# A two-layer graph attention kernel: scoring and summing layer 0's large units in two parts

## Chip, cores and metric

The kernel runs on one core of a Trainium2 chip. The metric is device microseconds (us) of one execution, from start to end on that core. Of the kernel before, nine timed runs are known: median 2654.25 us, from 2637.88 to 2664.31 us.

## What is computed

Two graph attention layers over 2048 nodes, for 8 batches with 256 channels each. `adj` is a symmetric 0/1 matrix with ones on its diagonal, the same for all batches. Layer 0, cut to what matters:

```
h1, h2, h3 = x @ W1, x @ W2, x @ W3
e = leaky_relu(h1 @ h2.T, 0.2);  e = where(adj > 0, e, -1e12)
x = layernorm(x + relu(softmax(e) @ h3))
```

Layer 1 has four heads, whose logits are the sum of a source and a destination term, the same mask and softmax, an elu, a residual and a layernorm. The change touches layer 0.

## The kernel before

**Lists.** The kernel sorts the nodes by degree, takes them 128 at a time (a group `t` of 16), and lists each node's neighbours. A group has as many slots as its largest node has neighbours: `SLOTS = (36, 24, 22, 21, 20, 19, 19, 18, 17, 17, 16, 15, 15, 14, 13, 12)`. Where a node has fewer neighbours than its group has slots, the index points out of range and `neg` holds -3e38 for that slot (0 otherwise).

**Units.** A unit is one group for one half of the batches (four batches, `HB`). There are 32 units per layer, 298 slots per half and 596 per layer. Layer 0 takes the groups from 12 slots up to 36, first for one half and then for the other. For each slot an indirect DMA on the GpSimd queue (POOL, line 196) gathers 128 rows of 1024 floats, the neighbour's features for four batches, into a ring of 16 buffers with two slots each (`RING`, `CHUNK`).

**Layer 0, per unit.**
- `before0` (from line 530): the unit's own rows, transposed and multiplied by W1 W2ᵀ, give `g`.
- `logits0` (from line 552): for each slot and batch one instruction on VectorE (DVE, line 568) multiplies the gathered row with `g` and adds up to one logit in `e`. After a part's last slot there follow leaky relu (581), the mask added from `neg` (582), maximum (586), subtraction (587), the exponential on ScalarE (ACT, 588), sum (591), and, for a unit with one part, reciprocal and normalisation (593, 594).
- `sums0` (from line 654): for each slot ACT builds four 128x64 diagonal matrices from the weights (665; four sets of buffers), and TensorE (PE) multiplies them with the gathered rows into two PSUM accumulators (645). After a slot pair's sum its ring buffer is free again. `evict` copies the accumulators to `hs` with ACT (680), during the next unit's first slot.
- `after0` (from line 695): `hs` is transposed, multiplied by W3, added to the residual (DVE, 705), and DVE's statistics (384) go to ACT's logarithm and exponential (395, 396), DVE's factors (397 to 403) and ACT's normalisation (407). PE then transposes the result and projects it for layer 1.

A unit of more than 24 slots (only that of 36) was already scored and summed in two parts of 18, each with a maximum and sum of its own; `shares` (from line 600) worked out two factors after both, and `evict` weighted both accumulators with them (686, 689).

**Order of the work.** A loop over units (from line 978) emits one slot's sum after another and calls `tick` after each. A tick starts gathers as far as ring buffers are free, then takes up to two steps of the scoring stream, then steps of the list, start and finish streams. Two rules hold scoring back: a row is scored at the earliest three ticks after its gather was issued (line 563), and scoring goes on only while the slots that are scored and not yet summed, `ahead`, are fewer than the limit in line 998: what is left of this unit, plus the whole next unit, plus `LEAD` (5).

```
tick(left + units[min(j + 1, len(units) - 1)].K + LEAD)
```

The order of POOL's queue is the one written down; on the other engines a scheduler may move instructions. Each engine works its queue in order.

Of the kernel before, what the change touches and what calls it, by code (L numbers as in the profile page):

```python
# [11 lines left out]
F32 = mybir.dt.float32  # L12
# [4 lines left out]
AF = mybir.ActivationFunctionType  # L17
# [19 lines left out]
SLOTS = (36, 24, 22, 21, 20, 19, 19, 18, 17, 17, 16, 15, 15, 14, 13, 12)  # L37
CHUNK = 2
RING = 16
LEAD = 5  # L40
LATE = 6

# [87 lines left out]
def fast_path(  # L130
# [51 lines left out]
    def ps_tile(name):  # L182
        return ps.tile([P, 512], F32, tag="ps", name=name)
# [254 lines left out]
    class Unit:  # L438
        def __init__(self, layer, h, t):
            self.layer, self.h, self.t = layer, h, t  # L440
            self.K = SLOTS[t]
            self.name = f"{layer}_{h}_{t}"

            n = self.K if self.K <= RING * CHUNK * 3 // 4 else -(-self.K // 2)
            self.parts = [(k, min(n, self.K - k)) for k in range(0, self.K, n)]
            self.chunks = [[] for _ in self.parts]
            self.p = [None] * len(self.parts)
            self.ps = [None] * len(self.parts)

            self.m, self.s = [], []  # L450
            self.xo = None
            self.ready = False
# [99 lines left out]
    def logits0(u):  # L552

        while not u.ready:
            yield 0
        for i, (k0, K) in enumerate(u.parts):
            n, o = f"{u.name}_{i}", offs[u.t] + k0
            e = ep.tile([P, HB, K], F32, tag="e", name=f"e_{n}")
            for k in range(K):
                c, s = divmod(k, CHUNK)  # L560
                while len(u.chunks[i]) <= c:
                    yield 0
                while clock[0] < u.chunks[i][c][2] + 3:
                    yield 0
                rows = u.chunks[i][c][0]
                for b in range(HB):
                    jt = sp.tile([P, C], BF16, tag="j", name=f"j_{n}_{k}_{b}", bufs=4)
                    nc.vector.tensor_tensor_reduce(  # L568
                        out=jt,
                        in0=rows[:, s, ts(b, C)],  # L570
                        in1=u.g[:, ts(b, C)],
                        scale=1.0,
                        scalar=0.0,
                        op0=ALU.mult,
                        op1=ALU.add,
                        accum_out=e[:, b, k : k + 1],
                    )
                yield 1
            p = e
            wide = [P, HB, K]  # L580
            nc.vector.scalar_tensor_tensor(p, e, ALPHA, e, ALU.mult, ALU.max)
            nc.vector.tensor_tensor(
                p, p, neg[:, o : o + K].unsqueeze(1).to_broadcast(wide), ALU.add
            )
            m = sp.tile([P, HG], F32, tag="m1", name=f"m_{n}")[:, :HB]
            nc.vector.tensor_reduce(m, p, AX.X, ALU.max)
            nc.vector.tensor_tensor(p, p, m.unsqueeze(2).to_broadcast(wide), ALU.subtract)
            nc.scalar.activation(p, p, AF.Exp)
            yield 0
            sm = sp.tile([P, HG], F32, tag="s1", name=f"s_{n}")[:, :HB]  # L590
            nc.vector.tensor_reduce(sm, p, AX.X, ALU.add)
            if len(u.parts) == 1:
                nc.vector.reciprocal(sm, sm)
                nc.vector.tensor_tensor(p, p, sm.unsqueeze(2).to_broadcast(wide), ALU.mult)
            u.m.append(m)
            u.s.append(sm)
            u.p[i] = p
            yield 0

    def shares(u, G):  # L600


        f = sp.tile([P, 2, HG], F32, tag="f", name=f"f_{u.name}", bufs=1)[:, :, :G]
        top = sp.tile([P, HG], F32, tag="top", name=f"top_{u.name}", bufs=1)[:, :G]
        nc.vector.tensor_tensor(top, u.m[0], u.m[1], ALU.max)
        for i in range(2):
            nc.vector.tensor_tensor(f[:, i, :], u.m[i], top, ALU.subtract)
        nc.scalar.activation(f, f, AF.Exp)
        for i in range(2):
            nc.vector.tensor_tensor(u.s[i], u.s[i], f[:, i, :], ALU.mult)  # L610
        nc.vector.tensor_tensor(top, u.s[0], u.s[1], ALU.add)
        nc.vector.reciprocal(top, top)
        nc.vector.tensor_tensor(f, f, top.unsqueeze(1).to_broadcast([P, 2, G]), ALU.mult)
        fs = sp.tile([P, 2, 2, HG // 2], F32, tag="fs", name=f"fs_{u.name}", bufs=1)
        fs = fs[:, :, :, : G // 2]
        for r in range(2):
            rr = slice(64 * r, 64 * r + 64)
            pf = ps_tile(f"ps_f_{u.name}_{r}")[:, :G].rearrange("p (i g) -> p i g", i=2)
            for c in range(2):
                nc.tensor.matmul(  # L620
                    pf[64 * c : 64 * c + 64],
                    lhsT=ident[rr, rr],
                    rhs=f[rr, :, ts(c, G // 2)],
                    start=True,
                    stop=True,
                    tile_position=(64 * r, 64 * c),
                )
            nc.vector.tensor_copy(fs[:, :, r, :], pf)
        return fs
# [23 lines left out]

    def sums0(u):
        accs = []
        for i, (k0, K) in enumerate(u.parts):
            while u.p[i] is None:
                yield 0
            acc = [acc_tile(f"acc_{u.name}_{i}_{r}") for r in range(2)]
            for k in range(K):  # L660
                c, s = divmod(k, CHUNK)
                rows, n, _ = u.chunks[i][c]
                diag = dp.tile([P, HB, 64], F32, tag="dg", name=f"dg_{u.name}_{i}_{k}")
                for b in range(HB):
                    nc.scalar.activation(  # L665
                        diag[:, b, :], twice, AF.Copy, scale=u.p[i][:, b, k : k + 1]
                    )
                while evictions:
                    evictions.popleft()()
                add_slot(acc, k, K, rows[:, s, :], diag)  # L670
                if s == n - 1:
                    credits[0] += 1
                yield 1
            accs.append(acc)

        def evict():
            u.hs = hsp.tile([P, HC], F32, tag="hs", name=f"hs_{u.name}")
            if len(accs) == 1:
                for r in range(2):
                    nc.scalar.copy(u.hs[:, ts(r, HW)], accs[0][r])  # L680
                return
            fs = shares(u, HB)
            for r in range(2):
                for j in range(2):
                    v = u.hs[:, ts(2 * r + j, C)]
                    nc.scalar.activation(
                        v, accs[0][r][:, ts(j, C)], AF.Copy, scale=fs[:, 0, r, j : j + 1]
                    )
                    nc.vector.scalar_tensor_tensor(
                        v, accs[1][r][:, ts(j, C)], fs[:, 1, r, j : j + 1], v, ALU.mult, ALU.add  # L690
                    )

        evictions.append(evict)

# [266 lines left out]
    def tick(limit):  # L961
        pump()
        while late and late[0][0] <= clock[0]:
            late.popleft()[1]()
        for _ in range(2):
            if ahead[0] < limit:
                ahead[0] += next(stream, 0)
        for queue in queues:
            for _ in range(min(len(queue), 2)):
                if queue and next(queue[0], queue) is queue:  # L970
                    queue.popleft()
        clock[0] += 1
# [5 lines left out]
    for j, u in enumerate(units):  # L978
        begun = False
        if 0 < j and j + 2 < NT:  # L980
            lists.append(neighbours(up[j + 2]))
        if j == NT:
            ends.append(checks())
        while len(ends) > 1:
            tick(0)
        if 2 <= j < 10:
            b, i = divmod(j - 2, 2)
            n = ts(i, N // 2)

            nc.gpsimd.dma_start(xg[1][n, ts(b, C)], x[HB + b, n])  # L990
        if j + 3 < 2 * NT:

            own_rows(units[j + 3])
        left = float(u.K)
        for share in sums[u.layer](u):
            ahead[0] -= share
            left -= share
            tick(left + units[min(j + 1, len(units) - 1)].K + LEAD)
            if not begun and left <= u.K / 2 and j + 3 < len(units):
                begun = True  # L1000
                v = units[j + 3]
                starts.append(before[v.layer](v))
        ends.append(finish(u))
# [300 lines left out]
```

## Time and profile before

One execution was profiled. Its own time was 2661.76 us; the span from its first to its last instruction was 2660.0 us. Layer 0's first score falls shortly after 160 us and its last sums shortly before 1560 us.

| engine | busy us | share of the span |
|---|---|---|
| PE | 2106.8 | 79% |
| DVE | 2012.4 | 76% |
| POOL | 1516.1 | 57% |
| ACT | 1443.2 | 54% |

The DMA engines moved 734.92 MB, 276 GB/s on average; 70.7% of their span went to the queue of the indirect gathers and scatters. TensorE's granted clock was 0.872 of full speed on average.

How to read it: shares are averages over a set-up, two layers with different work and a short end. In layer 0 DVE's main row is line 568, in layer 1 it is line 846. A wait is put down to the instruction or transfer that ended last before it.

### The profile page before, as it was taken

Reading aid. Unit: us, or ns where it says so; the run is one execution under the profiler, and the core shown is the slowest. Engines: PE = TensorE matmul, PEld = TensorE weight load, DVE = VectorE, ACT = ScalarE, POOL = GpSimd, SP = SyncE. Lnnn points to the kernel's source line nnn. Section 1 sums busy time; section 2 is a strip of 40 time slices with the busy share of each in tenths; the row PEclk is TensorE's granted clock in tenths of the full one; section 3 lists DMA queues with packets and bytes.
Section 4 is the critical chain, followed back from the end, with each engine's and each line's share of the span. In section 5 each row is a group of like instructions: output and inputs, shape, how many; then the busy total and the mean of one; then the engine's idle time right before and its main releaser. Section 6 shows DMA issues by size and latency. Waiting matters only on the chain.

```text
span 2660.0 us, 52177 instructions
## 1 busy us (share of the span) xinstructions
PE 2106.8 (79%) x16675; PEld 1112.3 (42%) x16675; DVE 2012.4 (76%) x7073; ACT 1443.2 (54%) x4849; POOL 1516.1 (57%) x1486
## 2 busy tenths in 40 slices
PE   0147888898899889888989878877787788787885
PEld 0135555555555556555655533223323222223332
DVE  7679687777878667677778667778867787787886
ACT  6135565655567556766666765432455545542544
POOL 3454455545466445555555646666666666665663
PEclk9578889888899899999999988887879889788887
DMA  9777788888786677888988678887889899867882
GB/s 380 275 261 249 269 292 281 266 273 270 248 285 227 208 236 267 282 294 270 306 289 270 234 249 298 317 290 263 292 318 313 295 321 322 300 245 271 330 303 93
DMA packets 249419, 734.92 MB, mean 276 GB/s; under 512 B 63200, under 2 KB 72544, under 8 KB 246704
## 3 DMA queue, kind: packets, MB, share of 16 engines
q0 software_dynamic: 192512, 645.89, 70.7%
q1 hardware_dynamic: 55360, 84.44, 9.3%
q8 instruction: 135, 2.21, 0.3%
q10 hardware_dynamic: 1264, 1.18, 0.1%
q14 instruction: 148, 1.21, 0.1%
HBM read 708.35 MB, written 76.09 MB: 295 GB/s over the span
## 4 chain that ended last, share of the span: by engine, by line
PE 30%; issue 27%; DVE 15%; DMA 12%; POOL 10%; ACT 3%; another core or an unknown queue 1%; POOLq 1%; DVEq 0%; SPq 0%; ACTq 0%
PE acc L645 26%; DVE j L568 8%; DMA s<-xg,idx 8%; POOL s L196 7%; DMA s<-qg,idx 3%; DVE s L846 2%; DMA nb<-edges,order 1%; PE ps_p_h L427 1%; ACT dg L665 1%; PE ps_p_g L427 1%; DVE st L384 1%; POOL qg L204 1%; DVE y L705 1%; PE ps_q L729 1%; POOL out_dram L204 1%
## 5 line engine op out<-in xcount | busy, mean ns | idle before, releaser
L568 DVE CUSTOM_DVE_ANT_0 j<-s,g 128x256 bf16<-128x256 f32 x2384 | 857.8, 420 | 258.4 <-DMA s<-xg,idx 209.7
L645 PE MATMUL acc<-s,ident 64*64 64x512 f32 x4768 | 856.5, 678 | 208.1 <-issue 177.5
L196 POOL DMA_INDIRECT s<-xg,idx x596 | 626.1, 1050 | 591.5 <-PE acc L645 318.0
L645 PE MATMUL acc<-s,dg 64*64 64x256 f32 x9536 | 752.1, 414 | 127.6 <-ACT dg L665 56.0
L196 POOL DMA_INDIRECT s<-qg,idx x596 | 603.4, 1012 | 345.9 <-issue 147.5
L665 ACT ACTIVATE dg<-twice,e 128x64 f32<-128x64 f32 x2384 | 623.3, 337 | 167.0 <-PE acc L645 101.3
L645 PEld LDWEIGHTS acc<-s,ident 64*64 64x64 f32 x4768 | 319.3, 150 | 734.5 <-issue 675.4
L645 PEld LDWEIGHTS acc<-s,dg 64*64 64x64 f32 x9536 | 402.9, 142 | 415.0 <-issue 176.6
L846 DVE TENSOR_TENSOR s<-s,p 128x2048 f32<-128x2048 f32 (+1 forms) x260 | 574.3, 2230 | 0.0
L842 ACT ACTIVATE s<-s,e 128x64 f32<-128x64 f32 x1408 | 345.2, 335 | 64.8 <-issue 23.6
L780 DVE TENSOR_TENSOR e<-s,own 128x32 f32<-128x32 f32 (+1 forms) x306 | 56.8, 187 | 218.8 <-DMA s<-qg,idx 188.8
L568 DVE DVE_READ_ACCUMULATOR2_ANT e<- 128x1 f32 x2384 | 192.3, 81 | 5.4 <-issue 5.4
L395 ACT ACTIVATE z<-st,roots 128x4 f32<-128x4 f32 x64 | 19.1, 298 | 310.5 <-DVE st L384 220.5
L204 POOL DMA_INDIRECT out_dram<-o,oidx x128 | 129.7, 1013 | 66.9 <-issue 31.6
L427 PE MATMUL ps_p_g<-A,xT 128*128 128x256 f32 x512 | 135.3, 410 | 27.3 <-ACT xT L419 24.9
L729 PE MATMUL ps_q<-wqs,x1T 128*128 128x264 f32 x512 | 138.3, 404 | 8.7 <-issue 2.3
L427 PE MATMUL ps_p_h<-w_sb,hT 128*128 128x256 f32 x512 | 130.6, 398 | 2.6 <-issue 1.8
L427 PEld LDWEIGHTS ps_p_g<-A,xT 128*128 128x128 f32 x512 | 99.5, 203 | 58.4 <-ACT xT L419 28.0
L729 PEld LDWEIGHTS ps_q<-wqs,x1T 128*128 128x128 f32 x512 | 96.5, 196 | 40.3 <-issue 12.5
L796 ACT ACTIVATE e<-e 128x288 f32<-128x288 f32 (+11 forms) x34 | 14.8, 435 | 181.1 <-DVE e L795 73.1
L427 PEld LDWEIGHTS ps_p_h<-w_sb,hT 128*128 128x128 f32 x512 | 93.9, 193 | 40.4 <-issue 18.1
L407 ACT ACTIVATE o<-xr,nmr,rstd 128x256 f32<-128x256 f32 x128 | 66.4, 589 | 81.6 <-DVE nmr L403 28.2
(138 smaller groups left out, 1484.8 us busy)
## 6 DMA issues: line engine op xcount, KB each, us to landing
adj<-in_adj_dram SPq DMA_DIRECT2D x16, 1024.0 KB
xr<-xo SPq DMA_DIRECT2D x128, 128.0 KB
x1s<-y SPq DMA_DIRECT2D x32, 512.0 KB
xr<-x1s SPq DMA_DIRECT2D x32, 512.0 KB
s<-xg,idx POOLq DMA_INDIRECT x596
s<-qg,idx POOLq DMA_INDIRECT x596
edges<-adj SPq DMA_DIRECT2D x16, 512.0 KB
xg<-in_x_dram SPq DMA_DIRECT2D x4, 2048.0 KB
```

The costliest lines, as they stand in the source:

```text
L196: nc.gpsimd.indirect_dma_start(out=dst, out_offset=None, in_=table, in_offset=AT(ap=index, axis=0), bounds_check=table.shape[0] - 1, oob_i ...
L204: ins = nc.gpsimd.indirect_dma_start(out=table, out_offset=AT(ap=index, axis=0), in_=src, in_offset=None)
L384: nc.vector.bn_stats(st[:, i, :], y[:, 2 * i : 2 * i + 2, :].rearrange("p b c -> p c b"))
L407: nc.scalar.activation(dst[:, b, :], y[:, b, :], AF.Identity, bias=nmr[:, b : b + 1], scale=rstd[:, b : b + 1],)
L427: nc.tensor.matmul(pp[:, ts(j, C)], lhsT=srcT[:, ts((2 * i + j) * KC + k, P)], rhs=weight[:, k, :], start=(k == 0), stop=(k == KC - 1),)
L568: nc.vector.tensor_tensor_reduce(out=jt, in0=rows[:, s, ts(b, C)], in1=u.g[:, ts(b, C)], scale=1.0, scalar=0.0, op0=ALU.mult, op1=ALU.add, ...
L645: nc.tensor.matmul(out, lhsT=lhsT, rhs=rhs, start=(k == 0 and j == 0), stop=(k == K - 1 and (j == 1 or diag is None)), tile_position=(64 * ...
L665: nc.scalar.activation(diag[:, b, :], twice, AF.Copy, scale=u.p[i][:, b, k : k + 1])
L729: nc.tensor.matmul(pq[:, : C + 2 * H], lhsT=x1T[:, ts(i * KC + k, P)], rhs=w.sqs[:, k, j * H : j * H + CD + H], start=(k == 0), stop=(k == ...
L780: nc.vector.tensor_tensor(e[:, c * CHUNK : c * CHUNK + ns, :].rearrange("p s (b g) -> p s b g", b=HB), rows[:, :ns, :].rearrange("p s (b w ...
L842: nc.scalar.activation(v[:, a, g, :], v[:, a, g, :], AF.Copy, scale=pv[:, a, g : g + 1])
L846: nc.vector.tensor_tensor(v, v, pv.unsqueeze(3).to_broadcast([P, n * HB, H, D]), ALU.mult)
```

## The change

Layer 0's units of `SPLIT` = 16 slots or more (11 of 16 groups, 22 of 32 units) get two parts of about half the slots, the first an even number: 12+12, 12+10, 10+11, 10+10, 10+9, 10+8, 8+9, 8+8; the unit of 36 keeps 18+18, so 20 units are newly split. Layer 1's parts stay.

The mask is no longer added by an instruction of its own: the score's instruction takes `neg`'s column of that slot as the start value of its sum, a [128, 1] operand in SBUF where 0.0 stood. This holds for all units of layer 0.

The second part's tile `e` has a column ahead of its logits, into which the first part's maximum is copied. It takes part in the second part's maximum, subtraction and exponential, so that it becomes the factor of the first part. Its product with the first part's sum goes into a column behind the logits and is added with them; then factor and weights of the second part are normalised together. The first part's weights are never normalised: its accumulators are multiplied with the factor, which four small matmuls and two copies on ACT (`spread_shares`) bring into the accumulators' layout. That multiplication is done by ACT in the midst of the second part's sums, and `evict` adds the second part's accumulators on DVE.

The limit of `ahead` now counts parts: what is left of this part, plus the next part, plus 5.

```diff
-            n = self.K if self.K <= RING * CHUNK * 3 // 4 else -(-self.K // 2)
-            self.parts = [(k, min(n, self.K - k)) for k in range(0, self.K, n)]
+            n = self.K
+            if layer == 0 and n >= SPLIT:
+                n = CHUNK * ((n + 2) // (2 * CHUNK))
+            elif n > RING * CHUNK * 3 // 4:
+                n = -(-n // 2)
+            self.parts = [(0, n), (n, self.K - n)][: 1 if n == self.K else 2]
...
-            e = ep.tile([P, HB, K], F32, tag="e", name=f"e_{n}")
+            last = i == len(u.parts) - 1
+            e = ep.tile([P, HB, 1 + K + 1], F32, tag="e", name=f"e_{n}")
...
-                        scalar=0.0,
+                        scalar=neg[:, o + k : o + k + 1],
...
-            nc.vector.scalar_tensor_tensor(p, e, ALPHA, e, ALU.mult, ALU.max)
+            p = e[:, :, 1 : 1 + K]
+            nc.vector.scalar_tensor_tensor(p, p, ALPHA, p, ALU.mult, ALU.max)
+            v = p
+            if i:
+                v = e[:, :, : 1 + K]
+                nc.vector.tensor_copy(e[:, :, 0], u.m[0])
+            m = sp.tile([P, HG], F32, tag="m1", name=f"m_{n}")[:, :HB]
+            nc.vector.tensor_reduce(m, v, AX.X, ALU.max)
             nc.vector.tensor_tensor(
-                p, p, neg[:, o : o + K].unsqueeze(1).to_broadcast(wide), ALU.add
+                v, v, m.unsqueeze(2).to_broadcast([P, HB, v.shape[2]]), ALU.subtract
             )
...
-            nc.scalar.activation(p, p, AF.Exp)
+            nc.scalar.activation(v, v, AF.Exp)
...
+            if i:
+                v = e[:, :, 1:]
+                nc.vector.tensor_tensor(e[:, :, 1 + K], e[:, :, 0], u.s[0], ALU.mult)
+            nc.vector.tensor_reduce(sm, v, AX.X, ALU.add)
+            if last:
                 nc.vector.reciprocal(sm, sm)
...
+                if i:
+                    u.fs = spread_shares(u, e)
...
+    def spread_shares(u, e):
+        fs = sp.tile([P, 2, 2], F32, tag="f0", name=f"f0_{u.name}", bufs=2)
+        for r in range(2):
+            rr = slice(64 * r, 64 * r + 64)
+            pf = ps_tile(f"ps_f0_{u.name}_{r}")[:, :2]
+            for c in range(2):
+                nc.tensor.matmul(
+                    pf[64 * c : 64 * c + 64], lhsT=ident[rr, rr], rhs=e[rr, ts(c, 2), 0],
+                    start=True, stop=True, tile_position=(64 * r, 64 * c),
+                )
+            nc.scalar.copy(fs[:, r, :], pf)
+        return fs
...
+                if i == 1 and k == 3:
+                    u.hs = hsp.tile([P, HC], F32, tag="hs", name=f"hs_{u.name}")
+                    for r in range(2):
+                        for j in range(2):
+                            nc.scalar.activation(
+                                u.hs[:, ts(2 * r + j, C)], accs[0][r][:, ts(j, C)], AF.Copy,
+                                scale=u.fs[:, r, j : j + 1],
+                            )
...
         def evict():
+            if split:
+                for r in range(2):
+                    v = u.hs[:, ts(r, HW)]
+                    nc.vector.tensor_tensor(v, v, accs[1][r], ALU.add)
+                return
...
+        ends_of = [u.K - k0 - K for k0, K in u.parts]
+        follow = [K for _, K in u.parts[1:]] + [units[min(j + 1, len(units) - 1)].parts[0][1]]
...
-            tick(left + units[min(j + 1, len(units) - 1)].K + LEAD)
+            i = next(i for i, end in enumerate(ends_of) if left > end or end == 0)
+            tick(left - ends_of[i] + follow[i] + LEAD)
```

More of the change, by code (lines that the diff above doesn't have):

```diff
@@ L39 @@
 RING = 16
+SPLIT = 16
 LEAD = 5
@@ L572, in logits0 @@
                         scale=1.0,
-                        scalar=0.0,
+                        scalar=neg[:, o + k : o + k + 1],
                         op0=ALU.mult,
                         op1=ALU.add,
-                        accum_out=e[:, b, k : k + 1],
+                        accum_out=e[:, b, 1 + k : 2 + k],
                     )
                 yield 1
-            p = e
-            wide = [P, HB, K]
-            nc.vector.scalar_tensor_tensor(p, e, ALPHA, e, ALU.mult, ALU.max)
+            p = e[:, :, 1 : 1 + K]
[6 more added lines that the diff above has]
+            nc.vector.tensor_reduce(m, v, AX.X, ALU.max)
             nc.vector.tensor_tensor(
-                p, p, neg[:, o : o + K].unsqueeze(1).to_broadcast(wide), ALU.add
+                v, v, m.unsqueeze(2).to_broadcast([P, HB, v.shape[2]]), ALU.subtract
             )
[L585 to L588, printed above, removed]
+            nc.scalar.activation(v, v, AF.Exp)
             yield 0
             sm = sp.tile([P, HG], F32, tag="s1", name=f"s_{n}")[:, :HB]
-            nc.vector.tensor_reduce(sm, p, AX.X, ALU.add)
-            if len(u.parts) == 1:
-                nc.vector.reciprocal(sm, sm)
-                nc.vector.tensor_tensor(p, p, sm.unsqueeze(2).to_broadcast(wide), ALU.mult)
+            v = p
+            if i:
[3 more added lines that the diff above has]
+            if last:
+                nc.vector.reciprocal(sm, sm)
+                v = p if i == 0 else e[:, :, : 1 + K]
+                nc.vector.tensor_tensor(
+                    v, v, sm.unsqueeze(2).to_broadcast([P, HB, v.shape[2]]), ALU.mult
+                )
+                if i:
+                    u.fs = spread_shares(u, e)
             u.m.append(m)
@@ L598, in logits0 @@
             yield 0
+    def spread_shares(u, e):
[5 more added lines that the diff above has]
+                nc.tensor.matmul(
+                    pf[64 * c : 64 * c + 64],
+                    lhsT=ident[rr, rr],
+                    rhs=e[rr, ts(c, 2), 0],
+                    start=True,
+                    stop=True,
+                    tile_position=(64 * r, 64 * c),
+                )
+            nc.scalar.copy(fs[:, r, :], pf)
+        return fs
     def shares(u, G):
@@ L655, in sums0 @@
         accs = []
+        split = len(u.parts) == 2
         for i, (k0, K) in enumerate(u.parts):
@@ L672, in sums0 @@
                     credits[0] += 1
+                if i == 1 and k == 3:
[5 more added lines that the diff above has]
+                                scale=u.fs[:, r, j : j + 1],
+                            )
                 yield 1
@@ L676, in evict @@
         def evict():
-            u.hs = hsp.tile([P, HC], F32, tag="hs", name=f"hs_{u.name}")
[L678 to L682, printed above, removed]
-            for r in range(2):
[L684 to L691, printed above, removed]
+            if split:
[3 more added lines that the diff above has]
+                return
+            u.hs = hsp.tile([P, HC], F32, tag="hs", name=f"hs_{u.name}")
+            for r in range(2):
+                nc.scalar.copy(u.hs[:, ts(r, HW)], accs[0][r])
         evictions.append(evict)
```

## Prediction

> **What bounds the kernel now.** I first looked at where layer 0 lies and how full its engines are. The view of busy times by stretch gives, for the start of the scoring and for the 1300 us that hold nearly all of layer 0 (columns: stretch, its length, then PE, PE's weight loads, DVE, ACT and POOL busy, granted clock, DMA share, GB/s):
>
> ```profile
> 160.00:200.00 40.00, 29.05 (x285) 19.20 (x285) 39.50 (x236) 22.57 (x80) 16.57 (x16) 0.80 0.67 219
> 200.00:1500.00 1300.00, 1137.42 (x10937) 720.68 (x10932) 996.54 (x5361) 813.49 (x2833) 689.00 (x660) 0.92 0.80 266
> ```
>
> PE is the fullest engine with 1137.4 of 1300 us, 87.5%; DVE has 996.5 (76.7%), the DMA engines 80%. No engine is full, so waits in the queues take the rest. At the start, from 160 to 200 us, DVE is full (39.5 of 40).
>
> Next the waits of that stretch (who waits, for whom, us in all, times, longest):
>
> ```profile
> POOL s L196 <- PE acc L645: 315.8, 158, 11.6
> DVE j L568 <- DMA s<-xg,idx: 208.4, 132, 6.1
> ...
> ACT z L395 <- DVE st L384: 95.9, 22, 7.5
> ...
> PEld acc L645 <- ACT dg L665: 86.8, 115, 5.7
> ACT e L588 <- DVE e L587: 79.9, 19, 9.9
> ```
>
> Read from top to bottom this is a ring. A gather waits for PE to free a ring buffer; DVE's score waits for that gather's rows; ACT, in order, waits at the exponential (79.9) and at the statistics (95.9) for a DVE that is behind with scoring; PE waits for ACT's diagonals (86.8); and PE's sum frees the next buffer. One turn of it shows in the timeline of ACT around 1330 us:
>
> ```profile
> 1332.20 0.30 ACT L395 ACTIVATE z<-st,roots 128x4 f32<-128x4 f32 x1 [7.34 <-DVE st L384]
> 1332.40 1.05 ACT L665 ACTIVATE dg<-twice,e 128x64 f32<-128x64 f32 x4
> ```
>
> For 7.34 us ACT made no diagonal, and in 1330 to 1340 us PE was busy 6.72 of 10 at a granted clock of 0.83, against 1.00 in the stretches on both sides.
>
> **The change, part by part.**
>
> *Distance between gather and score.* Before, a unit of 20 slots may be scored while fewer than 20 + 20 + 5 slots are ahead; the ring holds 32, so only the three-tick rule ever holds scoring back, and a row is scored as soon as that allows. After, the limit is at most 10 + 10 + 5 = 25 and falls to 15 as the part is summed: 7 to 17 of the ring's 32 slots are rows that had that long to land. Three ticks become 7 or more, for all split units. The 208.4 us of DVE waiting for rows should nearly go there (by the code's rules most of the 22 units of 16 slots and more had a distance near three). In the built order of ACT's queue, the exponential of a unit of 20 to 24 slots stands 1 to 3.75 slots ahead of its first diagonal before, and 11 to 14 after. What is late next is DVE's own work, or PE's.
>
> *The scalar operand.* All 2384 scores get a [128, 1] operand in the place of an immediate. No score with one is in the trace, so I bound it. Rows with immediates or none against rows with such an operand (last columns: busy us, mean ns of one):
>
> ```profile
> L568 DVE CUSTOM_DVE_ANT_0 j<-s,g 128x256 bf16<-128x256 f32 x2384 | 857.8, 420 | 258.4 <-DMA s<-xg,idx 209.7 <-issue 36.6 <-DVE e L568 4.7
> L846 DVE TENSOR_TENSOR s<-s,p 128x2048 f32<-128x2048 f32 x248 | 559.8, 2279 | 0.0
> ...
> L705 DVE SCALAR_TENSOR_TENSOR y<-ps_p_h,xr 128x512 f32<-128x512 f32 x64 | 43.7, 682 | 5.3 <-PE ps_p_h L427 4.3 <-PE acc L645 1.0
> ...
> L289 DVE TENSOR_SCALAR_CACHE_REDUCE junk<-keys,key 128x2048 f32<-128x2048 f32 x8 | 18.7, 2340 | 4.3 <-issue 4.3
> ...
> L846 DVE TENSOR_TENSOR s<-s,p 128x1024 f32<-128x1024 f32 x12 | 14.6, 1213 | 0.0
> ...
> L689 DVE SCALAR_TENSOR_TENSOR hs<-acc,fs,hs 128x256 f32<-128x256 f32 x8 | 3.3, 475 | 0.5 <-issue 0.5
> ```
>
> The two forms of line 846 give (2279 - 1213) / 1024 = 1.041 ns per element. Without its elements, line 846 has 147 ns left, line 705 149, line 568 153; lines 289 and 689, the two with a [128, 1] operand, both have 208. That is 55 to 61 ns more. Durations of neighbours overlap, so I also read starts:
>
> ```profile
> 897.46 0.41 DVE L568 CUSTOM_DVE_ANT_0 j<-s,g 128x256 bf16<-128x256 f32 x1
> 897.80 0.08 DVE L568 DVE_READ_ACCUMULATOR2_ANT e<- 128x1 f32 x1
> 897.80 0.42 DVE L568 CUSTOM_DVE_ANT_0 j<-s,g 128x256 bf16<-128x256 f32 x1
> 898.14 0.08 DVE L568 DVE_READ_ACCUMULATOR2_ANT e<- 128x1 f32 x1
> 898.14 1.65 DVE L689 SCALAR_TENSOR_TENSOR hs<-acc,fs,hs 128x256 f32<-128x256 f32 x4
> 899.71 0.41 DVE L568 CUSTOM_DVE_ANT_0 j<-s,g 128x256 bf16<-128x256 f32 x1
> ```
>
> Scores start 340 ns apart, the four of line 689 392 ns apart ((899.71 - 898.14) / 4), for 256 elements each: 52 more. The price lies between 0 (the score is another kind of instruction) and 61 ns; it can't be a gain, since the operand is one more thing to read. I take 55, nearest to both readings: 2384 x 55 = 131 us of DVE, 124 of it in the stretch (x2255 there). The Trainium skill, "Vector Engine (DVE) Microarchitecture Reference", "Measured stream behaviour on trn2", gives 1.0417 ns per column and about 75 ns per instruction after queue overlap for one- and two-source ops, with no word on a scalar operand; by it these 131 us would be 0 and rival B would hold.
>
> *Other DVE work.* Gone: 34 mask additions of about 0.22 us, 7.5 us. New in each of 20 units: leaky relu, maximum, subtraction and sum once more, about 0.2 each, a copy and a product of four columns, 0.16 each, and two additions of 512 columns from PSUM at 0.68 (row 705): 2.5 us, less 0.3 since the rows are shorter. 20 x 2.2 = 44. The unit of 36 loses its `shares` on both halves, 2 x 1.9. Sum 44 - 7.5 - 4 = about 33 us, 31 in the stretch.
>
> *ACT.* Per new split one more exponential (0.2), two small copies (0.25 each by the smallest rows), and four weighted 256-column copies at 475 ns for two plain ones at 583: about 1.45 us, 29 in all. ACT is 63% busy in the stretch and hides it; without that cover it would be 29 us.
>
> *PE.* Eight short matmul records per split (221 ns each, four at a time), some 0.5 us, 10 in all. PE now waits there for DVE's normalisation; behind it stand the current part's sums and the projections. By the built order the exponential is 7 slots earlier, so it waits only when DVE is that far behind.
>
> *New waits on DVE.* The additions in `evict` wait for PE's last sum of the unit; behind them stand the scores. With three `e` tiles and two per unit, a part's first score waits for ACT's last diagonal of the part three tiles earlier. Both cost nothing while DVE is behind PE, as it is now.
>
> *Sum.* DVE: 996.5 + 124 + 31 = 1152 us in the stretch, against PE's 1137 + 10. If the fullest engine were always busy, 1152 would be the floor; now it reaches 87.5% over the stretch, and 90.9% in the best 100 us of it (1200 to 1300 us, PE 90.89). Two engines nearly equally full wait for each other more, fewer row waits mean less; I take the middle, 89%: 1152 / 0.89 = 1294 us, 6 less than now. Before 200 us DVE is full already: some 65 scores x 55 ns = 4 us more. Layer 1 is left as it is. 2660 - 6 + 4 = 2658 us of span, 2 less; taken off the median of 2654.25 (the profiled execution's 2661.76 lies 7.5 above it), **2652 us**.
>
> **Rivals.** *A, the forecast:* the row waits go and DVE's extra work eats them. Fill from 87.5% (1317 us, +17) to 90.9% (1267, -33), with the 4 us: 2625 to 2675. For it: the two rows with 208 ns, and a DVE wait of 208 us against 155 us of added DVE work.
>
> *B, the operand costs nothing:* then DVE has 1028 us and PE with 1147 stays the fullest. Without row waits it should reach 90 to 93%: 1274 to 1233 us, 26 to 67 less; at 90.9% 1262, **2616**. For it: the score is no built-in form (CUSTOM_DVE). Against it: both readings above.
>
> *C, slower: DVE becomes the bound and its queue paces PE.* The same 1152 us of DVE work, but PE's queue now waits for DVE at `spread_shares`, DVE's for PE at the additions, and a DVE that can't run ahead (three `e` tiles) loses what it waits. It decides where DVE stays below 1152 / 1300 = 88.6% busy. At 84 to 87%: 1371 to 1324 us, 71 to 24 more; at 86% 1340, with the 4 us 44 more, **2698**. For it: units of 22 and more slots, where scores alone would take 88 x (346 + 55) = 35 us and more; against it: from 160 to 200 us DVE did reach 99%.
>
> That the change does not do what it says would show as row waits near 208 us; then C's upper end holds.
>
> **Chances.** About 0.5%, 13 us, is what a measurement of this kernel can tell from no change. A 0.44: faster by more than that 0.15, within it 0.20, slower 0.09. B 0.24: 0.23 faster, 0.01 same. C 0.32: 0.30 slower, 0.02 same. Together faster 0.38, same 0.23, slower 0.39. The range takes in A, most of B and C's nearer half, 2596 to 2704, and leaves out about 0.17. A's own range is 2625 to 2675.
>
> **What would show it.** The score's mean of 420 ns becomes 475 (A, C) or stays (B). DVE's wait for `s` rows in layer 0 falls from 208 to under 60 us; if not, the distance isn't what it seems. ACT's waits at the exponential and at the statistics fall by half or more; if they stay, DVE's own lateness made them, and C is near. DVE's share in layer 0 rises to 88% or more. The prediction is wrong if DVE is under 85% busy there with the operand's price paid, or if PE keeps its clock of 0.92 and is fuller than 92%.

## The result and the profile after

The changed kernel takes 2745.88 us (median of 10 runs, 2739.66 to 2753.66) beside 2651.88 us for the kernel before (median of 31). The ratio is 1.0359, interval [1.034, 1.0378]: 94 us slower where 2 us faster was forecast, and outside the range of 2596 to 2704. The profiled execution has a span of 2743.6 us, 83.6 more than before; the last transposes of `hs` begin at 1648.2 us, against 1565.1 before. So 83.1 of the 83.6 us are lost in layer 0.

Busy time by stretch, kernel after, the same stretches as in the prediction (length, then PE, PE's weight loads, DVE, ACT, POOL, clock, DMA share, GB/s):

```profile
160.00:200.00 40.00, 24.01 (x241) 16.16 (x241) 39.99 (x209) 19.34 (x70) 16.11 (x16) 0.80 0.66 217
200.00:1500.00 1300.00, 1093.55 (x10420) 686.97 (x10421) 1084.42 (x5143) 781.36 (x2748) 642.62 (x618) 0.92 0.76 251
```

In 1300 us PE is busy 1093.6 (it was 1137.4) and DVE 1084.4, 83.4% (76.7% before). The clock is 0.92 as before. No engine is full in it. A stretch of fixed length holds less of the work now, so layer 0 as a whole has to be compared. Before, it lies in 160 to 1566 us:

```profile
160.00:1566.00 1406.00, 1221.35 (x11801) 768.41 (x11805) 1068.59 (x5694) 880.60 (x3082) 743.72 (x713) 0.92 0.79 264
```

and after, in 160 to 1650 us:

```profile
160.00:1650.00 1490.00, 1239.25 (x11953) 773.11 (x11957) 1234.64 (x5807) 897.63 (x3183) 741.49 (x714) 0.92 0.75 249
```

DVE has 166 us more work (1234.64 - 1068.59); the prediction's 131 + 33 made 164. PE has 18 more, ACT 17 more. The work was counted nearly rightly (10 and 29 were forecast for PE and ACT). What fell is the fill: the fullest engine was busy 86.9% of layer 0 (PE, 1221 of 1406), and now it is 83.2% (PE, 1239 of 1490), with DVE beside it at 82.9%.

The score's row, after (busy, mean ns):

```profile
L575 DVE CUSTOM_DVE_ANT_0 j<-s,g,neg 128x256 bf16<-128x256 f32 x2384 | 993.7, 479 | 153.5 <-ACT dg L702 61.2
```

479 ns for 420: the [128, 1] operand costs 59 ns per score, 2384 x 59 = 141 us by these means. And the waits in 200 to 1500 us, after, less important rows left out (who waits, for whom, us in all, times, longest):

```profile
POOL s L198 <- PE acc L681: 364.0, 145, 9.5
...
PE ps_t_h L419 <- DVE hs L725: 87.7, 17, 9.3
ACT e L597 <- DVE e L594: 87.6, 27, 5.9
...
ACT z L397 <- DVE st L386: 63.8, 21, 7.7
DVE j L575 <- ACT dg L702: 61.2, 23, 13.2
ACT hT L421 <- PE ps_t_h L419: 58.5, 22, 7.9
DVE j L575 <- DMA s<-xg,idx: 50.8, 36, 6.1
...
PEld acc L681 <- ACT dg L702: 45.6, 81, 4.2
...
DVE y L743 <- PE ps_p_h L429: 29.2, 14, 5.7
```

DVE's wait for rows went from 208.4 to 50.8 us, as forecast. But the longest wait of a compute engine for another is new: PE waits 87.7 us at the transposes of `hs` for DVE's additions, up to 9.3 us at a time, and ACT waits 58.5 us behind that (`hT`). Also new is DVE waiting for ACT's last diagonals at a part's first score (61.2). The exponential's wait has not halved (87.6 for 79.9), that at the statistics is a third shorter (63.8 for 95.9), and PE's wait for diagonals is about half (45.6 for 86.8). The row waits have been exchanged for waits of PE, ACT and DVE on each other. How much time each of these waits costs, the rows alone don't say.

### The profile page after: what moved, and what is told of

Read it like the earlier page. It is cut to its first block, busy times and chain, and to the rows that moved or that the text cites. A ratio compares the mean times of both kernels' runs of the same rounds, so it can differ in the third digit from the quotient of the medians.

```text
span 2743.6 us, 52798 instructions
## 1 busy us (share of the span) xinstructions
PE 2118.3 (77%) x16835; PEld 1116.5 (41%) x16835; DVE 2181.1 (79%) x7183; ACT 1463.7 (53%) x4951; POOL 1511.5 (55%) x1486
## 5 line engine op out<-in xcount | busy, mean ns | idle before, releaser
L575 DVE CUSTOM_DVE_ANT_0 j<-s,g,neg 128x256 bf16<-128x256 f32 x2384 | 993.7, 479 | 153.5 <-ACT dg L702 61.2
L681 PE MATMUL acc<-s,ident 64*64 64x512 f32 x4768 | 847.4, 675 | 211.8 <-issue 172.1
L198 POOL DMA_INDIRECT s<-xg,idx x596 | 619.4, 1039 | 689.9 <-PE acc L681 399.5
L681 PE MATMUL acc<-s,dg 64*64 64x256 f32 x9536 | 762.9, 407 | 122.2 <-issue 61.7
L419 PE MATMUL ps_t_h<-ident,hs 128*128 128x128 f32 x256 | 53.0, 344 | 108.8 <-DVE hs L725 99.9
```

The costliest lines, as they stand in the source:

```text
L198: nc.gpsimd.indirect_dma_start(out=dst, out_offset=None, in_=table, in_offset=AT(ap=index, axis=0), bounds_check=table.shape[0] - 1, oob_i ...
L419: nc.tensor.transpose(pt[:, ts(j, P)], src[:, ts(4 * i + j, P)], ident)
L575: nc.vector.tensor_tensor_reduce(out=jt, in0=rows[:, s, ts(b, C)], in1=u.g[:, ts(b, C)], scale=1.0, scalar=neg[:, o + k : o + k + 1], op0= ...
L681: nc.tensor.matmul(out, lhsT=lhsT, rhs=rhs, start=(k == 0 and j == 0), stop=(k == K - 1 and (j == 1 or diag is None)), tile_position=(64 * ...
```

## The experiments

Each run stands beside runs of the kernel before on the same chip, in the same set. In some sets that kernel takes about 2650 us, in others about 2480 (the last section comes back to it), so ratios are compared, not times, and across sets with care: the changed kernel itself has 1.0359 in a set where the kernel before takes 2650 us and 1.0456 in one where it takes 2480. Of the runs below, before_dve_evicts, imm_act_evicts, imm_no_split and all_taken stand in a set of 2650 us, the others in sets of 2480; a comparison between the two kinds shows a direction better than a size. In the texts on record, theory L says that the operand's load on DVE is the loss, Q that the queues' couplings which the split makes are. Other letters stand for narrower readings of the same question. In the code cuts, `...` stands for parts of the edit that the text describes.

**imm_operand**: both parts, but an immediate in the score and the mask's own instruction.

```
-                        scalar=neg[:, o + k : o + k + 1],
+                        scalar=0.0,
...
```

> The changed kernel with one thing taken back: the score's start value is the immediate 0.0 again and the mask is added by its own instruction. That takes about 2384 x 59 ns = 141 us of work off VectorE and puts about 10 us back. Theory L (the operand's load on VectorE is what costs): 60 to 100 us faster than the changed kernel, 2645 to 2685 us, and TensorE's wait for the additions into hs falls from 100 us to under 40. Theory Q (the split's new waits between the queues cost, whatever the operand): only 10 to 40 us faster, 2705 to 2735 us, and the wait for the additions stays above 70 us.

2579.32 us, ratio 1.0384 [1.0347, 1.042], beside a kernel before of 2479.05, so the times expected can't be compared. Against changed_again below (1.0456, another set of 2480 us) the immediate gains 0.7%, some 17 us, and PE still waits 87.9 us at the transposes for the additions: both are Q's signs. Most of the loss is there without the operand.

**operand_alone**: the kernel before, with the operand and without the mask's instruction (the same edit the other way round).

> The kernel before with one part of the change alone: the score takes the mask's column as its start value and the mask's own addition goes; no unit is newly split. Theory L: VectorE lay on 16.7% of layer 0's chain with the scores, and it is now 59 ns longer per score; 50 to 90 us slower than the kernel before, 2702 to 2742 us. Theory Q: before, VectorE's waits for rows take most of it; 0 to 30 us slower, 2652 to 2682 us.

2511.62 us, 1.0119 [1.0083, 1.0156]. The score's mean was 478 ns in it, so about 130 us more of DVE work (2384 x 58 ns, less 7.5 us for the mask's instruction) cost about 33 us, between the two expectations. Most of it lies where DVE waited before: its wait for rows in 200 to 1500 us is 110.3 us here, and 200.5 in before_dve_load, which has the layer 0 of the kernel before. Alone, the operand makes about a third of the changed kernel's 3.6%.

One unit of imm_operand shows what the split does. PE, ACT and DVE around 1320 us, taken from three timelines (start, length, engine, line, in brackets the idle time ahead and what ended it); first PE:

```profile
1315.44 1.16 PE L770 MATMUL ps_q<-wqs,x1T 128*128 128x264 f32 x4
1322.17 1.09 PE L419 MATMUL ps_t_h<-ident,hs 128*128 128x128 f32 x4 [5.58 <-DVE hs L728]
```

then DVE:

```profile
1321.00 0.41 DVE L575 CUSTOM_DVE_ANT_0 j<-s,g 128x256 bf16<-128x256 f32 x1
...
1321.35 1.27 DVE L728 TENSOR_TENSOR hs<-hs,acc 128x512 f32<-128x512 f32 x2
```

and ACT:

```profile
1316.66 0.36 ACT L778 COPY q<-ps_q 128x264 f32<-128x264 f32 x1
1323.30 0.59 ACT L421 COPY hT<-ps_t_h 128x512 f32<-128x512 f32 x1 [6.28 <-PE ps_t_h L419]
```

From 1311.3 to 1321.3 us DVE did nothing but scores, one every 346 ns. The two additions that PE needs stood behind them in its queue and came at 1321.35. PE had the transposes of `hs` next and stood for 5.58 us, with the following sums behind them; ACT had the copy of these transposes next and stood for 6.28 us, with the diagonals for those sums behind it. In the same unit DVE afterwards waited 3.31 us for PE's projection, and ACT 6.32 us for DVE's subtraction. In the kernel before, ACT copies `hs`, and ACT is 63% busy there.

**e_room**: both parts' `e` of a unit in one of the three buffers, so that a part's first score doesn't wait for the diagonals of the part three tiles earlier.

```
-            e = ep.tile([P, HB, 1 + K + 1], F32, tag="e", name=f"e_{n}")
+            if i == 0:
+                both = ep.tile([P, HB * (u.K + 2 * len(u.parts))], F32, tag="e", name=f"e_{n}")
+            at = HB * (k0 + 2 * i)
+            e = both[:, at : at + HB * (K + 2)].rearrange("p (b k) -> p b k", b=HB)
```

> The changed kernel with room for three whole units of logits: both parts of a unit share one of the three buffers, so a part's first score no longer waits for the diagonals of the part three before (61 us of VectorE's waits in the changed kernel). Theory L: VectorE is short of time and uses it: 10 to 40 us faster than the changed kernel. Theory Q with the additions as the place: within 10 us of it, since VectorE would then wait for TensorE's last sum.

2624.27 us, 1.0574 [1.0536, 1.0612]. Neither theory expected it slower than the changed kernel (1.0456 in changed_again): DVE's waits for diagonals go, its waits for rows come back (183.5 us in 200 to 1600), and PE's at `hs` are 115.3 there. It fits that a DVE which may run further ahead puts more scores in front of the additions; that was not shown by itself.

**act_evicts**: as changed, but `hs` gets the second part's sums by a copy on ACT; the first part's sums are not added.

```
-                    nc.vector.tensor_tensor(v, v, accs[1][r], ALU.add)
+                    nc.scalar.copy(v, accs[1][r])
```

> The changed kernel with work left out: evict copies the second part's accumulators to hs with ScalarE, and the first part's weighted sums are not added. This takes 44 x 0.68 = 30 us off VectorE and puts 26 us on ScalarE, and TensorE's transposes of hs wait for ScalarE and not for a VectorE that is behind with scores. Theory Q: the 100 us of that wait go, 40 to 80 us faster than the changed kernel, 2665 to 2705 us. Theory L: the wait moves to the next point where VectorE is needed (statistics, exponential), 10 to 35 us faster.

2557.1 us, 1.0309 [1.0266, 1.0353]. PE's wait for DVE at `hs` is gone; ACT waits 303.4 us (46 times) at the exponential, as theory L expected.

**changed_again**: the changed kernel itself, as a mark for its set, that of the three runs below.

> The changed kernel itself, on the chip of the three runs beside it, since times differ between chips. If the split and the operand add up: the operand alone gave 1.012 of the kernel before and the split with the immediate 1.038, so about 1.05. If one covers the other: about 1.036, as first measured.

2598.22 us, 1.0456 [1.0422, 1.049], beside a kernel before of 2486.41. So split and operand don't quite add up (1.038 x 1.012 would be 1.050). Against it, act_evicts is 1.4% lower (1.0309 / 1.0456), some 36 us, about the upper end of L's 10 to 35 and under Q's 40 to 80. With the operand, taking the additions away leaves 3.1%.

**imm_old_limit**: both parts and an immediate, with the limit of `ahead` as it was.

```
-            tick(left - ends_of[i] + follow[i] + LEAD)
+            tick(left + units[min(j + 1, len(units) - 1)].K + LEAD)
```

> The split with the immediate, and with the old limit: scoring may run ahead by the rest of the unit, the whole next unit and 5, so rows are scored three ticks after their gather as before. Theory D (holding scoring back is what hurts: VectorE reaches a part's last score later than ScalarE reaches its exponential): 1.00 to 1.015 of the kernel before, and ScalarE's wait at the exponential falls from 202 us to under 120. Theory N (the number of exponentials and other meeting points hurts, wherever scoring stands): 1.03 to 1.045, with VectorE's row waits back above 150 us.

2608.73 us, 1.0497 [1.0466, 1.0527]. Holding scoring back is not the cause: without it the kernel is slower than imm_operand (1.0384) and no faster than changed_again. It lies above N's range, too, and DVE's wait for rows is 120.2 us, not above 150. PE now waits 134.0 us (17 times) at the factor's products for DVE's normalisation, where the changed kernel waits hardly at all (4.7 and 3.6 us).

**before_late_exp** and **split_late_exp**: the exponential of layer 0 three ticks after the subtraction, sum and normalisation four ticks after, in the kernel before, and in both parts with an immediate (its lines are shown).

```
+            tails.append((clock[0] + 3, lambda v=v: nc.scalar.activation(v, v, AF.Exp)))
+            tails.append((clock[0] + 4, weights))
...
```

> The kernel before, in which the exponential of layer 0 is emitted three ticks after the subtraction and the sum and normalisation four ticks after it. Nothing else changes. If ScalarE's waiting at the exponential, in order ahead of the diagonals, bounds the kernel: 0.975 to 0.99 of the kernel before, and that wait falls from about 80 us to under 30. If ScalarE then only waits at the statistics or VectorE's lateness moves on: 0.995 to 1.01.

> The split with the immediate, and with the exponential three ticks and the rest of the softmax four ticks after the subtraction. Theory E (the split hurts by doubling the points at which ScalarE waits in order for VectorE): 1.00 to 1.015 of the kernel before, with ScalarE's wait at the exponential under 60 us in layer 0. Theory H (the wait of TensorE for the additions into hs is the larger part): 1.025 to 1.04, with that wait at 90 us or more.

2486.58 us, 1.0000 [0.9981, 1.0019], and 2569.37 us, 1.0318 [1.0279, 1.0358]. Against 1.0384 the split gains 0.7% (the intervals overlap), the kernel before nothing. The edit did not shorten the wait that it aimed at: ACT waits 125.0 us at the exponential in before_late_exp, where the first reading expected under 30, and 196.3 in split_late_exp (202.2 in imm_operand). So the pair says little about that wait; PE's at the additions stays at 96.1 us, H's sign.

**imm_no_split**: the changed code with an immediate and `SPLIT` raised to 99, so that only the unit of 36 is in two parts.

> The changed kernel with the bound of the split raised so that only the unit of 36 slots is in two parts, and an immediate. If splitting the units of 16 to 24 slots is the cause of the loss: 0.995 to 1.005. If the rewritten code (the factor's place, the ahead limit, the layout of buffers) has a share: 1.01 or more.

2646.24 us, 0.999 [0.997, 1.0011]. The new limit, the layout of `e` and the factor for the unit of 36 cost nothing together. Splitting the units of 16 to 24 slots is the loss.

**before_dve_evicts**: the kernel before, with DVE instead of ACT copying `hs`.

```
-                    nc.scalar.copy(u.hs[:, ts(r, HW)], accs[0][r])
+                    nc.vector.tensor_copy(u.hs[:, ts(r, HW)], accs[0][r])
```

> The kernel before, with the sums of units in one part copied out of PSUM by DVE instead of ACT; nothing else. If DVE's place between PE's sums and PE's transposes of hs is a cause by itself: 1.015 to 1.03. If it only costs together with the split: under 1.005.

2693.36 us, 1.0179 [1.014, 1.0218]. No further unit is split, no score has the operand, 60 copies of 0.68 us change engine, and 46 us are lost. Its waits, 200 to 1500 us:

```profile
PE ps_t_h L417 <- DVE hs L680: 49.7, 13, 8.8
...
ACT hT L419 <- PE ps_t_h L417: 37.4, 22, 5.8
```

These are two of the changed kernel's new rows, made by one line in the kernel before. DVE is hardly fuller by it: 1003.13 of these 1300 us, and 997.65 in imm_no_split of the same set.

**imm_act_evicts** and **all_taken**: both parts, an immediate, ACT's copy of the second part's sums (the first part's are not added); and that with e_room's buffer and the late exponential as well.

> Both parts, an immediate in the first part's score (the mask instruction back), and hs copied out of the one PSUM group by ACT; this leaves out adding the first part's sums. By the split with an immediate (1.038) less what DVE's additions cost (about 0.015): 1.02 to 1.025 if the terms add. If the additions only cost where DVE is overfull with the operand, 1.035 or more.

> Split with an immediate, hs copied by ACT (leaves out adding the first part's sums), both parts' e in one buffer, layer 0's exp and normalisation later. If the meeting points of DVE, ACT and PE named so far are all of the loss: 1.00 to 1.015. If something else in the split has a share (more instructions, a second maximum and factor): 1.02 or more.

2671.59 us, 1.009 [1.006, 1.0119], and 2673.77 us, 1.0105 [1.0066, 1.0144]. With the additions gone and an immediate, some 0.9% are left of a loss that is 3.8% in imm_operand (a set of 2480 us): less than either reading expected. The buffers of `e` and the late exponential together change nothing in that. act_evicts (1.0309, a set of 2480 us) differs from imm_act_evicts by the operand alone, which would make the operand's price about 2% without the additions, for 1.2% by itself and 0.7% beside them. So the shares of operand and additions don't simply add.

**before_dve_load**: the kernel before, ACT copying, with two reductions of 512 elements on DVE beside each copy, which nothing reads.

```
+                    nc.vector.tensor_reduce(pad, w.w3[:], AX.XY, ALU.max)
```

> The kernel before, with ACT still copying hs, and two reductions of 512 elements more on DVE at the same place for each unit in one part, whose result nothing reads. If the copies by DVE cost 1.8% by DVE's added load: 1.012 to 1.02 here too. If they cost by DVE's place between PE's sums and PE's transposes: under 1.006.

2510.46 us, 1.0104 [1.0085, 1.0124], between the two ranges, but the run decides nothing. Where the reductions stand in the trace (minimum, median, maximum ns, then first and last start):

```profile
L682 DVE TENSOR_REDUCE pad<-w_sb x60: 672/686/687, 17.8 to 118.3; 128x1 f32<-128x512 f32 x60
```

As they use nothing of layer 0, the scheduler moved all 60 ahead to 17.8 to 118.3 us, where the lists are made. The load was never in layer 0.

**dve_evicts_late** and its control **before_late_hs**: `hs` copied by DVE and its transposes three ticks later in the order; and the same lateness with ACT copying.

```
+        for _ in range(3 if len(u.parts) == 1 else 0):
+            yield
         yield from transposed(hs, f"h_{n}", hT)
...
```

> The kernel before with hs copied by DVE, and the transposes of hs issued three ticks later in PE's queue, so that the sums of the next unit lie ahead of them. If PE's wait at these transposes is the price: under 1.008. If DVE's load, or the longer hold of the PSUM banks, is the price: 1.015 or more.

> The kernel before, ACT copying hs, with the transposes of hs of units in one part three ticks later: the control of dve_evicts_late, which had 0.997. If the later transposes pay by themselves, and DVE's copies cost nothing beside them: 0.994 to 0.998. If they pay nothing: 0.999 to 1.002.

2479.8 us, 0.9974 [0.9958, 0.9991], and 2474.58 us, 0.9952 [0.9935, 0.997]. The wait of PE in the first:

```profile
PE ps_t_h L417 <- DVE hs L680: 9.9, 6, 4.4
```

9.9 us for 49.7. DVE's copies cost 1.8% where PE needs them at once and about 0.2% (0.9974 / 0.9952, in two sets, intervals overlapping) where sums stand ahead of the transposes. The 1.8% come from a set of 2650 us, the 0.2% from sets of 2480, but what the kind of set changed in the changed kernel (3.6 or 4.6%) is small beside that. DVE has the same copies in both, so the price is their place and not their load. The control is also the fastest kernel of the study, half a per cent under the one before.

**imm_late_hs**: both parts, an immediate, DVE's additions, and the transposes of `hs` of split units three ticks later.

> Both parts with an immediate and DVE's additions, and the transposes of hs of units in two parts three ticks later in PE's queue. The split with an immediate had 1.038. If PE's wait for the additions is the price of their share: 1.01 to 1.025. If it is DVE's time on them, or the other waits take its place: 1.03 or more.

2541.87 us, 1.0239 [1.0215, 1.0263], for 1.0384. Nothing of the work is left out: 1.4%, some 36 us, goes by moving the transposes, and PE's wait at them falls from 87.9 to 19.3 us in 200 to 1500.

**imm_bare**: imm_act_evicts without the factor's products on PE and their copies, and without ACT's weighted copies of the first part's sums.

> Both parts with an immediate, ACT copying the second part's sums alone: the scaling of the first part's sums by ACT, the factor's two small products on PE and their copies are left out too. If these are the rest of the loss (1.009): 1.000 to 1.004. If the rest is in the scoring, the statistics in two steps and the smaller e: 1.006 to 1.01.

2481.63 us, 0.9993 [0.9977, 1.0009]. Scoring in two parts, with a second maximum, sum and exponential, costs nothing. What separates it from imm_act_evicts (1.009, in a set of 2650 us) are the factor and the first part's copies, 88 of 0.46 us on ACT. One row of it is worth a look (200 to 1500 us):

```profile
ACT e L600 <- DVE e L597: 266.7, 47, 9.6
```

ACT waits 266.7 us at the exponential here, 128.6 in before_dve_load of the same set, which has the layer 0 of the kernel before (79.9 in the profile before), and the time is that of the kernel before. This wait alone is no loss.

**imm_all_late**: both parts whole with an immediate; transposes three ticks later, late exponential, the factor's products issued behind the second part's first slot.

```
+                if i == 1 and k == 1:
+                    u.fs = spread_shares(u, u.e1)
...
```

> The split whole, with an immediate and DVE's additions, nothing left out; the transposes of hs three ticks later, layer 0's exp and normalisation 3 and 4 ticks after the subtraction, and the factor's products issued behind the first slot of the second part. The split with an immediate had 1.038 and 1.032 with the late exp, 1.024 with late transposes. If the split's loss is the meeting points in the queues and their placement takes it away: 1.00 to 1.012. If work that the split adds, or waits that come in the place of these, hold it: 1.018 or more.

2521.13 us, 1.0149 [1.0113, 1.0185], between what the two theories expected. PE's row at `hs` is nearly gone:

```profile
DVE j L577 <- ACT dg L709: 101.7, 27, 7.9
...
PE ps_t_h L419 <- DVE hs L734: 14.5, 6, 8.3
```

More than half of 3.8% was placement: the same work, issued elsewhere in the queues. DVE's wait for diagonals is larger than before the move (76.9 us in imm_operand). Which part of the remaining 1.5% is the first part's copies on ACT, the additions, or this wait, was not taken apart.

## Why the prediction was wrong, step by step

**Distance between gather and score: right, and worth little.** The row waits went (208.4 to 50.8 us), under the 60 that were named. But imm_bare, which scores at the new distance, waits 79.8 us for rows where before_dve_load, with the layer 0 of the kernel before, waits 200.5 in the same set, and takes the time of the kernel before; and all_taken (214.0 us) has the same time as imm_act_evicts (87.0). In imm_bare and imm_act_evicts DVE waits for diagonals instead (81.3 and 86.8 us). DVE's wait for rows was time that it had to spare.

**The operand: right in its size, 59 ns for the 55 taken.** Rival B is out. The Trainium skill, "Vector Engine (DVE) Microarchitecture Reference", "Measured stream behaviour on trn2", has no price for such an operand, and by its figures the score would have stayed as it was; the row decides. In time the operand is 1.2% by itself, and 0.7 to 2% beside the split, as above.

**Other DVE work: right.** 166 us more in layer 0, for 164 counted.

**New waits on DVE: the step that failed.** The prediction wrote that both "cost nothing while DVE is behind PE". It looked at DVE waiting for PE's last sum, and at what stands behind the additions. The price is on the other side: a DVE that is behind has scores in front of the additions, and PE waits for these at its next step, the transposes of `hs`. PE's wait there, of which the rows of before show none, is 87.7 us, and ACT's behind it 58.5. Moving the copy of `hs` from ACT to DVE does this without any of the rest (before_dve_evicts, 1.0179), and putting sums ahead of the transposes undoes it (dve_evicts_late, 0.9974). In the split with an immediate the same move takes 1.4 of 3.8% (imm_late_hs); what the wait costs in the changed kernel itself was not taken by itself.

**ACT "hides it": not quite.** The 29 us of ACT were costed at nothing. With the factor they are about 0.9% (1.009 against 0.9993, in sets of different kinds). Whether by ACT's time or by what waits behind its copies is open.

**PE at the factor: right.** In the changed kernel it waits there for DVE 8.3 us in all. With the old limit it was 134.0 (imm_old_limit, without the operand).

**Sum: the fill was the wrong kind of term.** 89% was taken since fewer row waits should mean a better fill. But a fuller DVE is not what costs: over layer 0, from 160 us to the last transposes of `hs`, DVE is busy 1177.70 of 1357 us (87%) in operand_alone and 1083.63 of 1427 (76%) in imm_operand, of the same set, and they take 1.0119 and 1.0384 of the time before. The fill here follows from who waits for whom, and the prediction had no term for PE waiting at `hs`. Its 89% was a choice between two values of the kernel before, whose waits are others. DVE stayed under 85% busy with the operand's price paid, which the prediction had named as a sign that it is wrong.

**Rival C: the right side, for half a reason.** It had PE waiting for DVE at the factor (8.3 us) and DVE waiting for PE at the additions, with DVE's fullness as the bound, and gave 44 us (71 at its end); the loss is 94, and the wait that was found runs the other way, PE for DVE's additions. The sign named for it, ACT's waits at the exponential and the statistics not halving, came true. With the operand's price taken away (imm_operand) the loss is still 3.8%, where the changed kernel has 4.6% in a set of the same kind. Placement in the queues makes more than half of these 3.8% (imm_all_late has 1.5%); what makes the rest stays open.

## What to carry to other kernels

When a step on the path between two engines is given to a third, ask what stands ahead of it in that engine's queue, not only what stands behind: 60 copies of 0.68 us cost 46 us on an engine that was 77% busy. If it must go there, put independent work of the waiting engine between (three ticks took the price from 1.8% to about 0.2%, in different sets). And before a wait is priced as gain, find who waits for the waiter: most of DVE's 208 us of row waits went, and nothing was gained by it.

## What the runs showed of the hardware

A [128, 1] operand in the place of an immediate makes the scoring instruction 59 ns longer (420 to 479 ns, 128x256), in operand_alone 58. The kernel before takes about 2650 us in two sets of runs and 2480 in four others, with the same bytes moved (734.92 MB). It is not the chip alone: two sets on the chip that the record calls 3 had 2647.76 and 2486.01. Much of it lies in layer 1: from the last transposes of `hs` to the end it is 1095 us in the profile before and 992 in before_late_hs. The kernel before, where it took 2661.76 us, in 1000 us of layer 1:

```profile
1600.00:2600.00 1000.00, 800.28 (x4378) 298.91 (x4374) 779.09 (x1047) 459.59 (x1565) 667.06 (x659) 0.83 0.85 298
```

and before_late_hs, in a set of the other kind, in 900 us of it:

```profile
1515.00:2415.00 900.00, 557.54 (x4426) 190.37 (x4418) 771.11 (x1043) 449.32 (x1544) 673.59 (x658) 0.82 0.90 330
```

With about the same instructions (4378 and 4426 on PE) PE counts as busy for 800 and 558 us at nearly the same granted clock, while DVE, ACT and POOL are busy for about as long in both. Layer 1's code is the same. One matmul is about as long in both (681 and 659 ns in the mean); busy time counts an instant once however many matmuls run in it, so they lie closer together in the second. Why was not tried.
